# Layer 0 of a two-layer image network: another order of TensorE's work around the turning of sums and norm factors

## The chip, the core and the metric

The kernel runs on one core of a Trainium2 chip. The core has a matrix engine (PE, TensorE), a vector engine (DVE), an activation engine (ACT, ScalarE), a general engine (POOL, GpSimd) and an engine that mostly issues transfers (SP). Each works through its own queue of instructions in order; between queues, semaphores order the work. Matmul results land in PSUM[...]; everything else lives in SBUF or in DRAM. The metric is the device time of one execution in microseconds; the time given for a kernel is the median of its runs.

## The reference

The input is eight images of 256 channels on 32 by 32 pixels. Layer 0, which the change touches, does for each image:

```
a = attention(norm(x))         # 4 heads, key width 32, value width 64, over 1024 pixels
    qkv  = conv1x1, scaled     # 512 output channels: q 128, k 128, v 256
    attn = softmax(q . k / sqrt(32))
    out  = v . attn + depthwise 3x3 of v, scaled
    a    = conv1x1(out), scaled
x = x + gamma1 * a
f = edffn(norm(x))
    1024 hidden channels by conv1x1, depthwise 3x3, gelu(first 512) * (last 512)
    conv1x1 back to 256 channels
    8x8 patches: rfft2, times a filter, irfft2
x = x + gamma2 * f
```

Here norm divides by the root of the mean square over channels. Layer 1 is a causal attention and a mixture of eight experts over the pixels as tokens; it takes the larger half of the time and is left as it is.

## The kernel before

All of layer 0 stays in float32. An image is held as channels on 128 partitions, two blocks of channels by 1024 pixels (tile `t`, three buffers, so that three images are in flight). PE's work for image i is written out by hand as a generator, `main_of(i)` (line 1137), and every PE, DVE, ACT and POOL instruction of it is recorded by a helper (`InOrder`, line 60) that keeps each engine in the order of the program. That is why nearly all lines of the profile say L72.

Three images overlap. While PE runs the attention of image i, it also mixes and transforms the hidden layer of image i-2 (`spectrum`, line 1065), normalises image i-1 for its feed-forward part (`norm2`, line 917), opens the hidden channel groups of image i-1 (`open_group`, tiles `ph`, `hpad`, `x`, `conv`) and makes queries, keys and values of image i+1 (`queries_keys`, line 720; `values`, line 753). `weave(main, side, every)` (line 1118) lets a step of one generator follow every so many steps of another.

DVE's work beside this is the depthwise convolutions, tap by tap: those of the hidden groups, and ahead of them that of the values, `v_conv` (line 783), which writes the tile `o` (one buffer): ACT writes its middle tap, DVE adds eight more taps to each of two blocks. `level` (line 460) puts these steps between those of `main_of`: as soon as the recorded PE time of this image, times a share (0.95 for most images), exceeds the recorded DVE time, DVE steps follow. An estimate in the program thus decides where in the order they stand.

The pieces that the change touches:

- `attend` (line 793): four chunks of 256 queries, each in four steps. A step makes the scores `s` of two key blocks, ACT takes their exp (`pT`), and PE multiplies the exps of the step before with the values (`po`) and with ones (`sums`).
- `close` (line 819): when a chunk ends, ACT copies `po` to `pu` and the sums to `ss`. Then follow three steps on PE: `turn` (transposes `tps`; DVE takes the reciprocal `sr`, ACT copies it, POOL splits it in two parts `rs`), `back` (transposes `trs`; ACT copies to `rsT`) and `spread` (matmul `rb`; DVE multiplies `pu` and adds it to `o`). `later` (line 857) takes one of them at each step. The last chunk's steps are left to `finish` (line 894).
- `project` (line 900): the output projection `pp` of `o`, in two halves of 512 pixels, and DVE's addition of it into `t`. The second half's result is in the small PSUM buffers `ps_m` (two of them), which most small matmuls share.
- `rms_norm` (line 619): ACT squares `t` (`sq`), PE forms the mean squares (`ms`), ACT adds the constant (`yr`), PE turns them (`tpy`), POOL computes the factor in seven instructions (`a`, `y`, `r`), and after some empty steps (`gaps`) PE turns it back (`tr`) and spreads it (`rbn`); DVE then multiplies (`xn`).
- `spectrum`: four mixing matmul groups (`pz`), ACT copies (`zf`), transforms (`pf`, DVE's product `gf`, `py`) and DVE's addition into `t`. After the last, SP stores the finished `t` (`td`) and loads image b+3 into the same buffer.
- `gelu_steps` (line 1041): ACT's gelu of four groups, each followed by DVE's product `hid`.

Of the kernel before, what the change touches and what calls it, by code (L numbers as in the profile page):

```python
# [2 lines left out]

# [6 lines left out]
F32 = mybir.dt.float32  # L10
F32R = mybir.dt.float32r
AF = mybir.ActivationFunctionType
# [5 lines left out]
P = 128  # L18
# [9 lines left out]
QC = 256  # L28
# [76 lines left out]
def conv_attn_hybrid_kernel(  # L105
# [369 lines left out]
    act, pool = InOrder(tc, nc.scalar), InOrder(tc, nc.gpsimd)  # L475
    t = [None] * B
    with ExitStack() as l0:
        wpool = l0.enter_context(tc.tile_pool(name="w0", bufs=1))
        one = l0.enter_context(tc.tile_pool(name="one0", bufs=1))
        two = l0.enter_context(tc.tile_pool(name="two0", bufs=2))  # L480
# [108 lines left out]
        accs = keep.tile([P, 2, B, N // QC], F32, name="accs")  # L589
# [119 lines left out]
        xn2 = {}  # L709
# [83 lines left out]
        def attend(b):  # L793

            qst, kst, vT = (att[b][n] for n in ("qst", "kst", "vT"))
            nj = NT
            todo = []

            def product(po, sm, j, pT):


                for pair in range(NH // 2):
                    for i in range(4):
                        ch = pair * P + i * KD
                        pe.matmul(
                            po[i * KD : (i + 1) * KD, pair, :],
                            vT[:, j, ch : ch + KD],
                            pT[:, ch // HD, :],  # L810
                            start=(j == 0 and pair == 0),
                            stop=(j == nj - 1 and pair == 1),
                        )
                for hd in range(NH):
                    pe.matmul(
                        sm[hd * KD : (hd + 1) * KD, :], ones[:, :KD], pT[:, hd, :], start=(j == 0), stop=(j == nj - 1)
                    )

            def close(c, po, sm):
                pu = two.tile([P, NH // 2, QC], F32, tag="pu", name="pu", bufs=1)  # L820
                act.copy(pu, po)
                ss = two.tile([P, QC], F32, tag="ss", name="ss", bufs=1)
                act.activation(ss, sm, AF.Copy, accum_out=accs[:, 0, b, c : c + 1])
                qs = slice(c * QC, (c + 1) * QC)
                nt = QC // P
                of = {}

                def turn():
                    tp = ps_m.tile([P, nt, P], F32, tag="mm", name="tps")
                    for i in range(nt):  # L830
                        pe.transpose(tp[:, i, :], ss[:, i * P : (i + 1) * P], ident)
                    r = small.tile([P, nt, NH], F32, tag="sr", name="sr", bufs=2)
                    dve.reciprocal(r, tp[:, :, ::KD])
                    flat = r.rearrange("p a b -> p (a b)")
                    act.activation(flat, flat, AF.Copy, accum_out=accs[:, 1, b, c : c + 1])
                    rs = of["rs"] = small.tile([P, nt, 2, NH], F32, tag="rsp", name="rs", bufs=2)
                    pool.tensor_copy(rs[:, :, 0, :].bitcast(F32R), r)
                    pool.tensor_sub(rs[:, :, 1, :].bitcast(F32R), r, rs[:, :, 0, :])

                def back():  # L840
                    tr = ps_m.tile([2 * NH, QC], F32, tag="mm", name="trs")
                    for i in range(nt):
                        pe.transpose(tr[:, i * P : (i + 1) * P], of["rs"][:, i].rearrange("p a b -> p (a b)"), ident)
                    of["rT"] = small.tile([2 * NH, QC], F32R, tag="rsT", name="rsT", bufs=1)
                    act.copy(of["rT"], tr)

                def spread():
                    rb = ps_m.tile([P, NH // 2, QC], F32, tag="mm", name="rb")
                    for pair in range(NH // 2):
                        pe.matmul(rb[:, pair, :], pick_r[:, pair, :], of["rT"], start=True, stop=True)  # L850
                    o = att[b]["o"][:, :, qs]
                    dve.tensor_mul(pu, pu, rb)
                    dve.tensor_add(o, o, pu)

                return [None, turn, back, spread]

            def later():
                if todo:
                    step = todo.pop(0)
                    if step:  # L860
                        step()

            late = []

            def products():
                for one_ in late:
                    product(*one_[:4])
                    if one_[2] == nj - 1:
                        todo.extend(close(one_[4], *one_[:2]))
                late.clear()  # L870

            for c in range(N // QC):
                qs = slice(c * QC, (c + 1) * QC)
                po = ps_o.tile([P, NH // 2, QC], F32, tag="po", name="po")
                sm = ps_o.tile([P, QC], F32, tag="sm", name="sums")
                for j0 in range(0, nj, 2):
                    new = []
                    for j in (j0, j0 + 1):
                        ks = slice(j * P, (j + 1) * P)
                        s = ps_s.tile([P, NH, QC], F32, tag="s", name="s")  # L880
                        for hd in range(NH):
                            pe.matmul(s[:, hd, :], kst[:, hd, ks], qst[:, hd, qs], start=True, stop=True)
                        pT = two.tile([P, NH, QC], F32, tag="pT", name="pT", bufs=4)
                        act.activation(pT, s, AF.Exp)
                        new.append((po, sm, j, pT, c))
                    products()
                    late.extend(new)
                    later()
                    yield 3.5
            products()  # L890
            att[b]["rest"] = todo
            yield 2.6

        def finish(b):
            for step in att[b]["rest"]:
                if step:
                    step()
                yield 0.4

        def project(b, halves):  # L900
            for h in halves:
                hs = slice(h * HALF, (h + 1) * HALF)
                if h == 0:
                    both = ps_s.tile([P, KC, HALF], F32, tag="s", name="pp")
                    pps = [both[:, g, :] for g in range(KC)]
                else:
                    pps = [ps_m.tile([P, HALF], F32, tag="mm", name="pp") for _ in range(KC)]
                for g in range(KC):
                    conv1x1(pps[g], projw, g * P, att[b]["o"], hs)
                    yield 1.7  # L910
                for g in range(KC):
                    tb = t[b][:, g, hs]
                    dve.scalar_tensor_tensor(tb, pps[g], proj_o[:, g : g + 1], tb, ALU.add, ALU.add)

        def norm2(b):
            xn2[b] = one.tile([P, KC, N], F32, tag="xn2", name="xn2")
            yield from rms_norm(b, "n2w", xn2[b], 2)
            ready2[b] = True  # L920

        def group_tile(n):
# [195 lines left out]
        def weave(main, side, every, rest=True):  # L1118

            for n, us in enumerate(main):  # L1120
                yield us
                if n % every == every - 1:
                    step = next(side, None)
                    if step is not None:
                        yield step
            if rest:
                yield from side

        def none():
            yield from ()  # L1130

# [5 lines left out]
        def main_of(i):  # L1137

            steps = attend(i)
            if i >= 1:
                if i == 1:
                    yield from weave(norm2(i - 1), steps, 2, rest=False)
                else:
                    mixing = spectrum(i - 2)
                    yield from weave(norm2(i - 1), mixing, 1, rest=False)
                    yield from weave(mixing, steps, 2, rest=False)
            yield from weave(steps, queries_keys(i + 1) if i + 1 < B else none(), 1)  # L1150
            gelus = gelu_steps(i - 1) if i >= 1 else none()
            if i + 1 < B:
                stack(i + 1)
                yield from weave(values(i + 1), finish(i), 1)
                yield from weave(project(i, (0, 1)), gelus, 1)
            else:
                yield from weave(project(i, (0,)), weave(finish(i), gelus, 1), 1)
                yield from project(i, (1,))
# [813 lines left out]
```

## Time and profile before

| | us |
|---|---|
| median of 3 runs | 3170.32 (3169.82 to 3171.17) |
| the profiled execution | 3171.4 |
| its span in the profile | 3169.4 |
| layer 0 within it | about 0 to 1400 |
| one image of layer 0 (distance of equal instructions) | about 164.5 |

Names in the profile are those of the program's tiles, so `trs<-ident,rs` is a transpose of `rs` into `trs`. "PEld" is the loading of matmul weights, which runs beside matmuls. A row of the timeline has start, duration, engine, line, operation, output and inputs, and the number of records; in brackets stands how long the engine had been idle before it and what ended that. A row of the waits says which engine waited with what for whom: total, times, longest. A row of the windows gives, for a stretch of time, the busy time of PE, PEld, DVE, ACT and POOL, the granted clock of PE (1.00 is full), the DMA engines' busy share and GB/s.

### The profile page before, as it was taken

The page shows a single profiled execution, that of the slowest core. Times are in us where ns is not written, and L with a number is a line of the kernel's source. Part 1 is how long each engine was busy: PE and PEld are TensorE (multiplying, and loading weights), DVE is VectorE, ACT ScalarE, POOL GpSimd, SP SyncE. Part 2 cuts the span into 40 slices and gives each one's busy share as a digit, 9 for nine tenths or more (in the row PEclk, how much of TensorE's full clock was granted, in tenths as well). Part 3 has the DMA queues.
Part 4 walks back from the last instruction along what each step waited for, and adds up shares of the span by engine and source line. Part 5 has one row for each costly group of instructions (what it writes and reads, how often), then busy time and mean ns, then how long its engine had stood idle before and what let it go on. Part 6 is the DMA issues. An engine that isn't in the chain of part 4 may idle for free.

```text
span 3169.4 us, 41581 instructions
## 1 busy us (share of the span) xinstructions
PE 2933.1 (93%) x16802; PEld 1936.7 (61%) x16802; DVE 2390.7 (75%) x3014; ACT 1564.5 (49%) x2312; POOL 343.9 (11%) x422
## 2 busy tenths in 40 slices
PE   5998899899898989868999999899999999999998
PEld 3654555455555555445666666677777777777776
DVE  1378877878787869675767665588988888888887
ACT  1554445555454536323333333365666666666664
POOL 1121211111111110001122222100000000000000
PEclk9998999999999999989999999999999999999999
DMA  5213030212112020002423221411112142211210
GB/s 152 56 26 80 28 81 27 70 38 58 50 41 68 28 67 1 25 28 85 163 107 120 106 103 67 186 67 67 67 67 94 60 175 97 80 67 67 100 67 28
DMA packets 63599, 234.86 MB, mean 74 GB/s; under 512 B 5590, under 2 KB 13606, under 8 KB 54566
## 3 DMA queue, kind: packets, MB, share of 16 engines
q1 hardware_dynamic: 63094, 230.54, 21.8%
q8 instruction: 134, 2.20, 0.3%
q0 software_dynamic: 304, 1.57, 0.1%
q14 instruction: 67, 0.55, 0.1%
HBM read 140.61 MB, written 91.49 MB: 73 GB/s over the span
## 4 chain that ended last, share of the span: by engine, by line
PE 77%; DVE 14%; ACT 3%; POOL 2%; DMA 2%; issue 2%; SPq 0%; ACTq 0%; DVEq 0%; POOLq 0%
PE pm L72 12%; PE pa L72 11%; PE q L72 11%; PE po L72 10%; PE s L72 8%; PE ph L72 6%; DVE conv L72 3%; PE pq L72 3%; PE sums L72 3%; DVE o L72 2%; PE pz L72 2%; PE pv L72 2%; PE pk L72 2%; DVE x L72 1%; DVE zt L72 1%
## 5 line engine op out<-in xcount | busy, mean ns | idle before, releaser
L72 PE MATMUL pa<-ze,w 128*128 128x512 f32 x1488 | 423.2, 393 | 0.0
L72 DVE SCALAR_TENSOR_TENSOR x<-hpad,vec,x 128x1024 f32<-128x1024 f32 x248 | 317.0, 1282 | 41.0 <-ACT x L72 34.0
L72 DVE SCALAR_TENSOR_TENSOR conv<-hpad,vec,conv 128x1024 f32<-128x1024 f32 x256 | 330.1, 1296 | 13.8 <-ACT conv L72 7.3
L72 PEld LDWEIGHTS pa<-ze,w 128*128 128x128 f32 x1488 | 278.2, 188 | 63.3 <-issue 3.1
L72 ACT ACTIVATE h<-pa,bn_o,s1a 128x512 f32<-128x512 f32 x256 | 198.6, 776 | 203.6 <-PE pa L72 203.6
L72 ACT ACTIVATE pT<-s 128x1024 f32<-128x1024 f32 x256 | 247.4, 1024 | 71.7 <-PE s L72 71.7
L72 PE MATMUL po<-pT,vT 128*32 128x256 f32 x4096 | 273.3, 385 | 0.0
L72 PE MATMUL q<-h2p,w 128*128 128x512 f32 x768 | 269.0, 459 | 0.0
L72 DVE SCALAR_TENSOR_TENSOR h<-pa,s1b,h 128x512 f32<-128x512 f32 x256 | 191.2, 747 | 93.8 <-PE pa L72 86.0
L72 PE MATMUL ph<-xn,piw 128*128 128x512 f32 x512 | 244.9, 616 | 3.1 <-DVE xn L72 1.6
L72 PE MATMUL pm<-h,w 128*128 128x512 f32 x512 | 240.9, 593 | 0.0
L72 PE MATMUL s<-kk,z 128*128 128x512 f32 x512 | 236.8, 594 | 4.1 <-DVE pr L72 4.1
L72 PE MATMUL q<-z_first,w 128*128 128x512 f32 x768 | 217.2, 391 | 2.7 <-DVE z_first L72 1.7
L72 PE MATMUL pm<-h1p,w 128*128 128x512 f32 x768 | 216.7, 390 | 0.5 <-DVE h1p L72 0.5
L72 DVE SCALAR_TENSOR_TENSOR o<-vpad,pe_w,o 128x1024 f32<-128x1024 f32 x128 | 163.5, 1282 | 45.6 <-ACT o L72 42.4
L72 PEld LDWEIGHTS q<-h2p,w 128*128 128x128 f32 x768 | 144.6, 188 | 83.2 <-issue 59.6
L72 PE MATMUL s<-qst,kst 128*128 128x256 f32 x1024 | 176.2, 314 | 14.6 <-DMA kst<-part 13.2
L72 ACT ACTIVATE hpad<-ph,pi_o 128x512 f32<-128x512 f32 x126 | 86.9, 689 | 183.1 <-PE ph L72 176.1
L72 PEld LDWEIGHTS po<-pT,vT 128*32 128x32 f32 x4096 | 120.6, 110 | 85.5 <-issue 3.7
L72 PEld LDWEIGHTS s<-qst,kst 128*128 128x128 f32 x1024 | 137.6, 193 | 47.9 <-issue 42.9
L72 PEld LDWEIGHTS q<-z_first,w 128*128 128x128 f32 x768 | 144.4, 188 | 34.4 <-DVE z_first L72 2.9
L72 PEld LDWEIGHTS pm<-h1p,w 128*128 128x128 f32 x768 | 144.7, 189 | 31.7 <-DVE h1p L72 0.9
(271 smaller groups left out, 5066.1 us busy)
## 6 DMA issues: line engine op xcount, KB each, us to landing
ze<-zd SPq DMA_DIRECT2D x29, 1536.0 KB, 6.3
qst<-part SPq DMA_DIRECT2D x32, 512.0 KB, 6.9
kst<-part SPq DMA_DIRECT2D x32, 512.0 KB, 14.6
te<-ud SPq DMA_DIRECT2D x32, 512.0 KB, 4.1
wd<-parts_w SPq DMA_DIRECT2D x20, 768.0 KB, 3.8
w<-wd SPq DMA_DIRECT2D x20, 768.0 KB, 5.6
zd<-parts SPq DMA_DIRECT2D x14, 1024.0 KB, 3.9
t<-in_x_dram SPq DMA_DIRECT2D x8, 1024.0 KB, 7.5
```

What stands on the lines that cost most here:

```text
L72: return self._tc.keep_in_program_order(method(*args, **kwargs))
```

## The change

It changes order only; no matmul, copy or transfer is added or removed. In `close` the copy of the sums precedes that of `po`, and the empty first step goes. `later` takes a flag: a chunk's first step (`turn`) now stands ahead of the products of its attention step, the other two behind them as before. `norm2` of images 1 to 6 gets five empty steps in place of two where it runs beside `spectrum`, and three elsewhere. At the end of image i, the gelus stand among and ahead of the values, and the projection's first half follows the turning of the last sums; its second half moves into the start of image i+1, behind one step of squares and one mixing step (for i+1 = 1, behind one attention step). There norm and mixing alternate by a new helper, `some(steps, n)`, which takes n steps of a generator.

```diff
             def close(c, po, sm):
+                ss = two.tile([P, QC], F32, tag="ss", name="ss", bufs=1)
+                act.activation(ss, sm, AF.Copy, accum_out=accs[:, 0, b, c : c + 1])
                 pu = two.tile([P, NH // 2, QC], F32, tag="pu", name="pu", bufs=1)
                 act.copy(pu, po)
-                ss = two.tile([P, QC], F32, tag="ss", name="ss", bufs=1)
-                act.activation(ss, sm, AF.Copy, accum_out=accs[:, 0, b, c : c + 1])
...
-                return [None, turn, back, spread]
-
-            def later():
-                if todo:
-                    step = todo.pop(0)
-                    if step:
-                        step()
+                return [turn, back, spread]
+
+            def later(first):
+                if todo and (len(todo) == 3) == first:
+                    todo.pop(0)()
...
+                    early = len(todo) == 3
+                    later(True)
                     products()
                     late.extend(new)
-                    later()
+                    if not early:
+                        later(False)
...
-        def norm2(b):
+        def norm2(b, gaps=3):
             xn2[b] = one.tile([P, KC, N], F32, tag="xn2", name="xn2")
-            yield from rms_norm(b, "n2w", xn2[b], 2)
+            yield from rms_norm(b, "n2w", xn2[b], gaps)
...
+        def some(steps, n):
+            for us in itertools.islice(steps, n):
+                yield us
...
                 if i == 1:
+                    yield from some(steps, 1)
+                    yield from project(i - 1, (1,))
                     yield from weave(norm2(i - 1), steps, 2, rest=False)
                 else:
-                    mixing = spectrum(i - 2)
-                    yield from weave(norm2(i - 1), mixing, 1, rest=False)
+                    mixing, second = spectrum(i - 2), norm2(i - 1, 5)
+                    yield from some(second, 1)
+                    yield from some(mixing, 1)
+                    yield from project(i - 1, (1,))
+                    for _ in range(3):
+                        yield from some(second, 1)
+                        yield from some(mixing, 1)
+                    yield from weave(second, mixing, 1, rest=False)
                     yield from weave(mixing, steps, 2, rest=False)
...
             if i + 1 < B:
                 stack(i + 1)
-                yield from weave(values(i + 1), finish(i), 1)
-                yield from weave(project(i, (0, 1)), gelus, 1)
+                steps, ends = values(i + 1), finish(i)
+                yield from some(gelus, 2)
+                yield from some(steps, 2)
+                yield from gelus
+                yield from some(ends, 1)
+                yield from project(i, (0,))
+                yield from some(steps, 2)
+                yield from some(ends, 1)
+                yield from some(steps, 1)
+                yield from ends
+                yield from steps
```

`project` and `v_conv` are unchanged, and so is `level`, which runs `main_of(i)` with the value convolution and the hidden groups as its side.

More of the change, by code (lines that the diff above doesn't have):

```diff
@@ L1 @@
+import itertools
 import math
@@ L895, in finish @@
             for step in att[b]["rest"]:
-                if step:
-                    step()
+                step()
                 yield 0.4
```

## The prediction

> **What bounds the kernel now.** I read the shares of the page first, then PE's waits over the four equal images from 500 to 1158 us, then one image stage by stage, then the instructions around each gap in order of time.
>
> ```profile
> PE 2933.1 (93%) x16802; PEld 1936.7 (61%) x16802; DVE 2390.7 (75%) x3014; ACT 1564.5 (49%) x2312; POOL 343.9 (11%) x422
> ...
> PE trs L72 <- POOL rs L72: 35.5, 8, 5.9
> PE tr L72 <- DVE gf L72: 13.0, 4, 3.2
> ...
> 500.00:523.00 23.00, 18.52 (x129) 13.33 (x128) 19.27 (x25) 6.44 (x8) 3.94 (x6) 0.93 0.11 46
> 523.00:546.00 23.00, 23.00 (x224) 12.53 (x225) 18.37 (x15) 15.68 (x24) 0.00 (x0) 1.00 0.13 47
> 546.00:562.00 16.00, 12.98 (x127) 7.35 (x126) 13.94 (x13) 7.16 (x12) 8.83 (x9) 0.89 0.01 1
> 562.00:623.00 61.00, 61.00 (x621) 35.18 (x624) 49.89 (x49) 35.18 (x54) 3.98 (x4) 1.00 0.17 52
> 623.00:643.00 20.00, 12.93 (x47) 6.14 (x40) 12.44 (x12) 5.70 (x13) 5.92 (x6) 0.83 0.77 161
> ...
> 505.02 0.38 PE L72 MATMUL tr<-ident,r 128*8 128x128 f32 x2 [3.24 <-DVE gf L72]
> 505.24 5.30 PE L72 MATMUL pz<-pow__116,hid 128*128 128x256 f32 x16
> 557.18 0.59 PE L72 MATMUL trs<-ident,rs 128*8 128x128 f32 x2 [3.02 <-POOL rs L72]
> 557.57 4.80 PE L72 MATMUL ph<-xn,piw 128*128 128x512 f32 x8
> 623.34 3.70 PE L72 MATMUL pq<-xn,qkvw 128*128 128x512 f32 x8
> 634.34 0.59 PE L72 MATMUL trs<-ident,rs 128*8 128x128 f32 x2 [5.87 <-POOL rs L72]
> 634.73 5.47 PE L72 MATMUL pq<-xn,qkvw 128*128 128x512 f32 x8
> ```
>
> PE is the bound of layer 0: in the long middle stage (562 to 623) it is busy for all 61.00 us. It idles in three places of an image, 3.24, 3.02 and 5.87 us; with seven waits of 0.7 us or less an image loses 15.2 us. After each of the three the next group is slower: pq 5.47 against 3.70 for the same eight records, ph 4.80 against 3.70, pz 5.30 (3.62 undisturbed). That adds some 1.8, 1.1 and 1.5 us (pz is 4.80 in another image), so an image gives away about 19.6 of its 164.5 us. DVE is busy four fifths of the image and waits for PE in between.
>
> Two other chains, which cost nothing now, matter for what follows:
>
> ```profile
> 655.16 2.38 ACT L72 ACTIVATE o<-vpad,pe_o,pe_w 128x1024 f32<-128x1024 f32 x2
> 656.50 6.57 DVE L72 SCALAR_TENSOR_TENSOR o<-vpad,pe_w,o 128x1024 f32<-128x1024 f32 x5 [2.42 <-ACT o L72]
> ...
> 518.80 0.88 DVE L72 SCALAR_TENSOR_TENSOR t<-py,vec,t 128x256 f32<-128x256 f32 x2 [0.96 <-PE py L72]
> 519.71 0.34 SPq L1114 DMA_DIRECT2D td<-t  x1
> 523.76 0.40 SPq L487 DMA_DIRECT2D t<-in_x_dram  x1
> 528.68 1.15 ACT L72 ACTIVATE sq<-t 128x512 f32<-128x512 f32 x2 [0.76 <-DMA t<-in_x_dram]
> ```
>
> The first is the opening of the value convolution: ACT writes o (1.19 us a half), then DVE adds taps (1.31 us each). The second is the recycling of the tile t: finished image out, next image in, 9.0 us from the last DVE add (519.68) to the squares that need it. ACT waits only 0.76 us for it.
>
> [...] granted clock 0.50 from 634.3 to 638.0. It shows the loss after 3.0 us of idling too. [...]
>
> **The change, part by part.** Times are from the start of an image's first value projection (623.34 in the trace).
>
> *Turning sooner (close, later).* The copies pu and ss swap: ss is done about 0.4 us sooner. tps goes ahead of the products, about 2.7 us sooner. In the trace the 3.02 us wait ends with POOL's chain, on which rs queues behind the eight microseconds of norm factors begun at 547.74. In the new order that norm starts one attention step sooner and tr stands ahead of trs: from tpy to trs PE has 17 us of work; the factors and rs need about 13. So 3.02 + 1.1 = **4.1 us saved**. If rs stays late, nothing.
>
> *Gelus and half the projection among the values.* PE now has pq (3.5), tps (0.2), pp half (3.4), tpv (0.5), pq (3.5) ahead of trs: it arrives at 11.2. DVE does four taps (to 3.9), three hid products (4.0, the third not before its gelu at 6.5), then the reciprocal at 8.1; ACT 8.6; POOL 0.85 + 1.25 us: rs at 10.8. The wait of 5.87 and its 1.8 us clock loss go; the margin is only 0.4 us. Small waits there and at pz, 1.9 us before, come to about 1.3 (rb after rsT 0.3, tpv after its copies 1.0). **Saved 8.2 us.** The tables loaded stay two an image; gelus cost ACT the same, in time that it had idle.
>
> *Second half of the projection after the first mixing step.* This is the costly edit. After that step `level` has spent PE time, so it starts v_conv before the projection: o has one buffer, and the order of instructions becomes: PE pp (second half, reads old o); ACT writes new o, waiting for that pp; DVE five taps on new o; only then DVE's adds of pp into t; then PE's ms, whose PSUM buffer is that pp's. PE therefore stands for 0.3 + 1.19 + 0.15 + 6.57 + 0.74 = **8.9 us, plus 1.8 us of slow clock: 10.7 lost**. Before, both adds stood ahead of the taps. DVE has nothing else ahead of these taps, and ACT's next squares queue behind the o copies. What could hide it: nothing on PE, which keeps program order.
>
> *norm2 with five gaps.* tr moves behind two more transforms and one pz. The factors are there 8.4 us after tpy (495.90, POOL's last r ends at 504.34), and gf has freed its buffer by then; PE now has 11 us of work between. The 3.24 + 1.5 go: **4.7 saved**. Behind it tr, pf, rbn and py follow each other closely on two PSUM buffers: I count waits of 0.6, 0.3, 0.4 and 0.3 us against 1.0 now: 0.6 lost. The last py now stands ahead of the scores instead of between them, so the exp is less covered: 0.8 lost.
>
> *Squares of the next norm, moved with the attention steps.* They now follow directly on the first two exps in ACT's queue. From the first score matmul: last add into t ends at +1.2; td and t take 9.0: +10.2. Behind it on ACT: two squares (1.06), two exps (1.93), hpad and x of ph (1.36): +14.5. PE's ms waits for that x, since it takes ph's buffer; PE arrives at 3.4 + 2.8 + 3.6 = +9.8. So 4.7 us of waiting, and some 1.5 of clock: **6.2 lost**. Then ms still holds one of two buffers while two ph groups come in one go: the second waits for hpad and x of the first: **1.6 lost**.
>
> Sum for images 2 to 6: saved 4.1 + 8.2 + 4.7 = 17.0; lost 10.7 + 1.4 + 6.2 + 1.6 = 19.9; **2.9 us slower each**. Followed from end to end instead (old and new position of the fourth attention step, less the 4.1), I get 2.2; I take 2.5: 12.5 us for five.
> - Image 2 loses a longer wait now, 7.20 (1.3 more saved). In images 2 and 6 the recycling took 10.9 us, so the new wait grows by 1.9, of which about 1 is paid now already: 1.8 lost.
> - Image 1: the wait at tpy (3.83), about 2 us of clock and 0.9 of small waits go; the o chain with four taps costs 7.6 + 1.8: 2.7 lost.
> - Image 7: no next image, so no squares wait: 12.5 saved, 12.7 lost (six taps).
> - Tail of image 7: the reciprocal no longer sits behind hid and adds; trs 3.82 and part of pp's 2.91 go: 3.1 saved.
>
> Total: 12.5 - 1.3 + 1.8 + 2.7 + 0.2 - 3.1 = 12.8 us lost. The profiled execution took 3171.4 (span 3169.4), the runs' median 3170.32; the difference is added to the median: **3183 us**. Layer 1 is untouched.
>
> Costs that the trace doesn't show: clock loss after each new wait, 0 to 2.3 us (taken 1.8 and 1.5); the trs margin, 0 to 2 us lost (taken 0); recycling of t, 9.0 to 10.9. A gain below these is excluded, since each only lengthens a wait.
>
> **Rivals.**
> 1. *The squares' wait doesn't bite* (faster). If t lands within 5.5 us of the first score matmul instead of 10.2, the 6.2 us go in five images, and PE gains 31: 3183 - 31 = **3152**. For: today ACT waits only 0.76 us, and PE not at all. Against: store and load each took 4.0 us or more, and the last add stands just ahead of the scores. It decides where a norm or transform ends some 4 us sooner than I count. Chance 0.25.
> 2. *Savings and losses cancel*: my two sums differ by 0.7 an image; 2.5 less an image gives **3170**. Chance 0.20.
> 3. *Worse*: the trs margin fails (2 us in six images) and each recycling takes 10.9 (3 more images by 1.9): 3183 + 12 + 6 = **3201**. For: margin 0.4. Chance 0.13.
> The turning in attention not doing what it is placed for (POOL still late) belongs to 3: 4.1 in five images.
>
> **Numbers.** Forecast 3183: 0.42. 0.2% (6.3 us) is what a measurement can tell from no change. Faster 0.25, same 0.20, slower 0.42 + 0.13 = 0.55. Range 3148 to 3202: below rival 1 and above rival 3 by their unknowns. The forecast's own range is 3176 to 3194.
>
> **What would show it.** Right: no wait of trs on rs near 6 or 3 us, none of tr on gf; instead PE ms waiting about 9 us for DVE t in images 2 to 7, DVE o waiting some 8 us for ACT o, ACT sq waiting 6 us or more for the load, PE ms some 5 us. Wrong: a period under 164 us per image, or ms without a wait: then o is not reopened where I read it, or the load is early.

## The result, and the profile after

| | us |
|---|---|
| before, median of 4 runs | 3170.07 (3163.39 to 3171.17) |
| changed, median of 4 runs | 3191.34 (3190.24 to 3192.97) |
| ratio | 1.0067, 95% interval 1.0055 to 1.0079 |
| span of the profiled execution, before and changed | 3169.4 and 3191.1 |

The change makes the kernel 21 us slower: inside the range on record (3148 to 3202), 8 us above the forecast. The waits of PE over images 3 to 6 (us 500 to 1158) of the changed kernel; columns are total, times, longest:

```profile
PE ms L73 <- DVE t L73: 35.0, 4, 8.8
PE ms L73 <- ACT x L73: 18.4, 4, 4.8
PE ph L73 <- ACT x L73: 5.8, 4, 1.4
PE tpv L73 <- ACT vT L73: 2.7, 4, 0.7
```

The two heads of the same list before, trs on rs (35.5) and tr on gf (13.0), are gone. In their place stand two waits of ms, of 8.8 and up to 4.8 us. PE's busy time on the page, in which slowed matmuls count with their longer time (four records of ph 3.78 us after one of the waits below, 1.98 elsewhere), is what it was (2933.0 against 2933.1). So the added time is time in which PE stands.

The first wait is read in the timeline, all engines, of the changed kernel (start, duration, engine, line, operation, tiles, records; in brackets the idle time before and what ended it):

```profile
494.75 3.60 PE L73 MATMUL pp<-o,projw 128*128 128x512 f32 x8
...
498.39 2.37 ACT L73 ACTIVATE o<-vpad,pe_o,pe_w 128x1024 f32<-128x1024 f32 x2 [2.85 <-PE pp L73]
499.73 6.57 DVE L73 SCALAR_TENSOR_TENSOR o<-vpad,pe_w,o 128x1024 f32<-128x1024 f32 x5 [6.36 <-ACT o L73]
506.21 1.40 DVE L73 SCALAR_TENSOR_TENSOR t<-pp,proj_o,t 128x512 f32<-128x512 f32 x2
507.10 1.08 PE L73 MATMUL ms<-sq,ones 128*32 128x128 f32 x16 [8.76 <-DVE t L73]
508.12 4.65 PE L73 MATMUL pz<-pow__116,hid 128*128 128x256 f32 x16
```

Read it downwards: pp ends at 498.3, ACT may then overwrite o, DVE runs five taps on the new o, and only then the two adds that free pp's PSUM. PE stands from 498.3 to 507.1.

The second wait, a little later in the same image:

```profile
532.45 0.34 SPq L1115 DMA_DIRECT2D td<-t  x1
...
536.34 0.40 SPq L488 DMA_DIRECT2D t<-in_x_dram  x1
...
542.05 1.15 ACT L73 ACTIVATE sq<-t 128x512 f32<-128x512 f32 x2 [7.71 <-DMA t<-in_x_dram]
543.11 1.92 ACT L73 ACTIVATE pT<-s 128x1024 f32<-128x1024 f32 x2
544.92 0.69 ACT L73 ACTIVATE hpad<-ph,pi_o 128x512 f32<-128x512 f32 x1
545.49 0.79 ACT L73 ACTIVATE x<-ph,dw_o,vec 128x512 f32<-128x512 f32 x1
546.15 0.70 ACT L73 ACTIVATE hpad<-ph,pi_o 128x512 f32<-128x512 f32 x1
546.33 1.08 PE L73 MATMUL ms<-sq,ones 128*32 128x128 f32 x16 [4.83 <-ACT x L73]
```

ACT waits 7.71 us for the load with exps and evacuations behind it in its queue; ms, which needs ph's buffer, waits 4.83 us for the x at 545.49.

To see where the 21.7 us between the two spans arise, take the first pf after both ms matmuls in the head of an image as a mark; at it both kernels have done the same work. The forecast's terms are sorted by the same cuts:

| stretch | forecast | measured |
|---|---|---|
| start to the mark in image 2's head (328.03, 348.48) | 2.7 - 9.5 + 10.7 = +3.9 | +20.5 |
| from there to the mark in image 7's head (1153.77, 1180.64) | 5 x 2.5 + 1.8 = +14.3 | +6.4 |
| from there to layer 1's first pk (1437.34, 1455.48) | the rest, -5.4 | -8.7 |
| layer 1 | 0 | +3.6 |

The last row is no effect of an edit: first to last pk takes 507.9 us before and 511.2 after, and in the profiles of the kernels below either 507.9 to 508.5 or 511.3 to 511.8, the fastest kernel (511.3) among the latter. What makes the difference is not known.

The surplus of the first row is in image 1. Rows of its timeline, changed kernel:

```profile
231.89 3.78 PE L73 MATMUL ph<-xn,piw 128*128 128x512 f32 x4 [4.04 <-ACT x L73]
...
276.11 0.63 PE L73 MATMUL rbn<-rT,pick_n 8*128 8x128 f32 x4 [3.19 <-DVE sr L73]
...
317.19 0.38 PE L73 MATMUL trs<-ident,rs 128*8 128x128 f32 x2 [2.66 <-POOL rs L73]
```

With an earlier wait of s (2.16, at 170.4) these are 12 us of waits that the forecast has not, where before showed one of 1.58. All four are followed by slower matmuls: the granted clock over the next 4 us was 0.50 after s and ph, 0.73 after rbn and 0.71 after trs (ph took 3.78 for four records, 1.98 elsewhere).

### The profile page after: what moved, and what is told of

The parts are those of the page before. It is cut to its first block, busy times and chain, and to the rows that moved or that the text cites. A ratio compares the mean times of both kernels' runs of the same rounds, so it can differ in the third digit from the quotient of the medians.

```text
span 3191.1 us, 41551 instructions
## 1 busy us (share of the span) xinstructions
PE 2933.0 (92%) x16802; PEld 1944.7 (61%) x16802; DVE 2393.0 (75%) x3014; ACT 1563.0 (49%) x2312; POOL 324.6 (10%) x422
## 4 chain that ended last, share of the span: by engine, by line
PE 78%; DVE 13%; DMA 3%; ACT 3%; issue 1%; POOL 0%; SPq 0%; ACTq 0%; DVEq 0%; POOLq 0%
PE pm L73 12%; PE pa L73 11%; PE q L73 11%; PE po L73 10%; PE s L73 8%; PE ph L73 5%; PE pz L73 3%; PE pq L73 3%; DVE conv L73 3%; PE sums L73 3%; DVE x L73 3%; PE pv L73 2%; PE pk L73 2%; DVE o L73 2%; PE pp L73 2%; DVE zt L73 1%
## 5 line engine op out<-in xcount | busy, mean ns | idle before, releaser
L73 PE MATMUL s<-qst,kst 128*128 128x256 f32 x1024 | 186.1, 326 | 19.5 <-DMA kst<-part 13.3
L73 PEld LDWEIGHTS s<-qst,kst 128*128 128x128 f32 x1024 | 144.2, 202 | 63.1 <-issue 49.0
L73 PEld LDWEIGHTS ph<-xn,piw 128*128 128x128 f32 x512 | 90.8, 191 | 121.1 <-issue 87.5
```

The costliest lines, as they stand in the source:

```text
L73: return self._tc.keep_in_program_order(method(*args, **kwargs))
```

## The experiments

Twelve kernels were run in three groups, each beside the kernel before on the same chip (its medians there: 3172.79, 3170.34 and 3170.78 us). Ratios are to the kernel before, with the 95% interval. The changed kernel itself was not run again in these groups; a difference to its 3191.34 is therefore uncertain by some 3 us, by which the medians of the kernel before differ.

### The two new waits, one at a time and together

e1 lets the value convolution in only when the adds are queued:

```
                                         # in hidden():
     on_dve = [n for n in range(2 * ng) if n not in on_pe]
+    while b not in projected:
+        yield None
     for i, us in enumerate(lead):
...                                      # at the end of project()'s loop:
+    if h == 1:
+        projected.add(b)
```

> The changed kernel, but the value convolution of image i (ACT's write of o and the first taps) is let in only when both adds of the second projection half are in DVE's queue; nothing is left out. Theory A (the adds stand behind o's taps, and PE's ms behind the adds): the waits of ms on t of 7.4 to 10 us go in images 1 to 7, with some 1.8 us of slow clock each, so about 70 us: 3120. Theory B (DVE only starts its taps later, and the time comes back as waits of ph on x or of pz on hid): 3165 to 3180. Theory C (the ms wait is no cause, what slows the change is the wait of the next norm's squares for the load): 3185 to 3195.

e2 starts the next image's norm one attention step later:

```
-weave(steps, queries_keys(i + 1) if i + 1 < B else none(), 1)
+weave(steps, later_on(int(1 < i), queries_keys(i + 1)) if i + 1 < B else none(), 1)
```

> The changed kernel, but the next image's norm begins one attention step later in images 2 to 6; nothing is left out. Theory A: ACT's wait for the load of t no longer stands ahead of the x that frees ph's buffer, the ms wait on x of 4.7 us and its slow clock go in five images: 3160 to 3165. Theory B (the wait moves: the norm's factors or the queries come late at the end of the attention instead): 3180 to 3195.

e3 has both edits:

> Both edits together. Theory A, the two waits are independent: the gains of the two runs add, near 3090 to 3100, some 70 to 80 us faster than the kernel before. Theory B: less than the larger of the two single gains, since the same time is hidden once only.

e4 puts the second half of the projection back into its own image:

```
-yield from some(steps, 1)           # in the head of image 1
-yield from project(i - 1, (1,))     # in the heads of images 1 and of 2 to 7
...
 yield from steps                    # the end of values(i + 1)
+yield from project(i, (1,))
```

> The changed kernel, but the second half of the projection stands at the end of its own image again, behind the values, not in the head of the next; all else of the change stays. Theory A (the split of the projection over the image's border is the costly edit, because the value convolution opens between pp and its adds): the long ms waits go, a new wait of pp on DVE's o of 2 to 3 us comes, about 3140. Theory B: the place of the second half matters little, 3180 to 3195.

| | median | ratio |
|---|---|---|
| e1 | 3159.89 | 0.9963 (0.9951 to 0.9976) |
| e2 | 3184.71 | 1.0040 (1.0025 to 1.0054) |
| e3 | 3153.64 | 0.9947 (0.9930 to 0.9963) |
| e4 | 3166.39 | 0.9982 (0.9971 to 0.9993) |

Reopening o between pp and its adds is a cause: without it the changed kernel becomes faster than the one before. But e1 gained 31 us, not 70. PE's waits of e1 over all of layer 0 (us 60 to 1440), and DVE and PE around one of them:

```profile
PE py L73 <- DVE gf L73: 24.3, 12, 4.8
PE ms L73 <- ACT x L73: 23.4, 5, 5.0
```

```profile
488.93 10.53 DVE L73 SCALAR_TENSOR_TENSOR o<-vpad,pe_w,o 128x1024 f32<-128x1024 f32 x8 [2.06 <-ACT o L73]
...
499.37 0.68 DVE L73 TENSOR_TENSOR gf<-pf,filt 128x512 f32<-128x512 f32 x1
...
500.11 2.08 PE L73 MATMUL py<-idft,gf 128*128 128x128 f32 x8 [3.64 <-DVE gf L73]
```

No ms wait on t is left (61.3 us in seven in the changed kernel), but the taps must run somewhere. Eight of them now stand ahead of gf, and py waits: 24.3 us in twelve waits, against 1.4 in the changed kernel. Theory A is right about the cause; the time came in below theory B's range, but part of it does come back, as B says, though at py and not at ph or pz. The marks show where: e1 is 19.9 us ahead at the mark in image 2's head (328.63), gains 5.4 us an image from there to image 7's head, and gives 11.8 us back behind that.

e2 removed the ms wait on x altogether and gained only 7 us. In its place, images 3 to 6:

```profile
PE ms L73 <- DVE t L73: 35.0, 4, 8.8
PE trs L73 <- POOL rs L73: 19.1, 4, 4.8
```

The time is theory B's, by a wait that it didn't name. The wait of trs in attention is back, and longer than before the change (3.02): the norm's factors again stand on POOL ahead of the sums' split. That wait had gone because the norm began early, which is what made ACT wait for the load. With the norm one step earlier or later, one of the two waits is there. The gains of e1 and e2 do add (38 us in e3), but each is far smaller than theory A of e3 took it (3090 to 3100).

e4 lies between its two theories. The long ms waits are gone and pp waits for o as foreseen (2.1 us an image), but tr waits for gf again: 12.9 us in four waits of images 3 to 6, as before the change. Of the 25 us to the changed kernel, all are there at the mark in image 2's head (322.97); from there to image 7's head e4 gains only 0.5 us an image.

### The start of image 1, and the turning alone

e5 restores the border between images 0 and 1:

```
 if i == 1:
-    yield from some(steps, 1)
-    yield from project(i - 1, (1,))
     yield from weave(norm2(i - 1), steps, 2, rest=False)
...
 yield from steps                    # the end of values(i + 1)
+if i == 0:
+    yield from project(i, (1,))
```

> The changed kernel, but at the border between images 0 and 1 the second half of the projection stays at the end of image 0, and image 1 begins with its norm, as before; nothing is left out. In the changed kernel's trace image 1 lost some 16 us that the prediction didn't count: waits of ph on x (4.0), rbn on sr (3.2), s (2.2), trs on rs (2.7). Theory A: they come from the moved half (DVE begins its taps early and the hidden groups bunch): they go together with the first ms wait (7.4) and its slow clock, 3170 to 3175. Theory B: they come from turning sooner or from the new end of image 0, only the ms wait goes and the wait at tpy (3.8) returns: 3185 to 3188.

3180.5 us, ratio 1.0032 (1.0021 to 1.0044), between the two theories. Its mark in image 2's head is at 336.21, 12.3 us ahead of the changed kernel's. The waits of rbn on sr and of s are gone, ph's on x and trs's shrink to 1.4 and 0.6, and the wait at tpy (3.8) is back; new are 2.8 of ph on pu and 5.0 of pz on hid. So moving the half projection over this border causes most of image 1's surplus, by the hidden groups' order behind it as well as by o: e1, without the o wait, still shows ph waiting 4.0 and rbn 3.2.

e7 is the changed kernel with close and later as before; e12 is the kernel before with the new close and later:

```
 def close(c, po, sm):               # e12; e7 is the reverse
-    act.copy(pu, po)
     act.activation(ss, sm, ...)
+    act.copy(pu, po)
...
+early = len(todo) == 3
+later(True)
 products()
 late.extend(new)
-later()
+if not early:
+    later(False)
```

> The changed kernel, but sums are copied and turned in attention as before (pu ahead of ss, tps behind the products and one step later); the rest of the change stays. Theory A (turning sooner itself saves the wait of trs on rs that the kernel before had in attention): a wait of 3 to 5 us returns in five images, 3205 to 3215. Theory B (the wait went because the next norm begins sooner, and its factors are through POOL before the sums are turned): no trs wait returns, 3185 to 3195.

> The kernel before with one edit of the change alone: sums copied and turned sooner. Nothing is left out. Theory A (turning sooner brings rs sooner and saves the wait of trs of 3.0 us in attention with its slow clock): 3145 to 3155. Theory B (POOL's queue decides: rs still stands behind the norm's factors, PE only arrives at trs earlier, and the wait stays or grows to the 4.8 us of the changed kernel with later squares): 3168 to 3182.

e7: 3189.48 us, ratio 1.0060 (1.0043 to 1.0076): the same time as the changed kernel, and no wait of trs in attention in images 2 to 6. e12: 3181.34, ratio 1.0029 (1.0019 to 1.0038): turning sooner alone makes the kernel slower. Both are theory B. POOL's queue there, with DVE's reciprocal and PE, e12:

```profile
714.11 2.53 POOL L72 TENSOR_TENSOR a<-y,mhalf 128x8 f32<-128x8 f32 x1 [43.41 <-ACT y L72]
715.05 0.20 DVE L72 RECIPROCAL sr<-tps 128x8 f32<-128x8 f32 x1
716.72 2.32 POOL L72 TENSOR_TENSOR y<-y,a 128x8 f32<-128x8 f32 x2
...
724.53 1.11 POOL L72 TENSOR_TENSOR rs<-sr,rs 128x8 fp32r<-128x8 f32 x1
...
725.70 0.59 PE L72 MATMUL trs<-ident,rs 128*8 128x128 f32 x2 [4.63 <-POOL rs L72]
```

The reciprocals are ready for POOL at 716.1, when ACT has copied them; rs starts at 724.27, when seven instructions of the norm's factors are through. Turning sooner does not make rs ready sooner; PE only comes to trs earlier and waits 4.63 us in place of 3.02.

### The other two parts alone

e8 is the kernel before with the new end of an image, and both halves of the projection in it:

```
-yield from weave(values(i + 1), finish(i), 1)
-yield from weave(project(i, (0, 1)), gelus, 1)
+steps, ends = values(i + 1), finish(i)
+yield from some(gelus, 2)
+yield from some(steps, 2)
+yield from gelus
+yield from some(ends, 2)            # the empty first step, and turn
+yield from project(i, (0,))
+yield from some(steps, 2)
+yield from some(ends, 1)
+yield from some(steps, 1)
+yield from ends
+yield from steps
+yield from project(i, (1,))
```

> The kernel before with the change's order at the end of an image alone (gelus and the first half of the projection among the values, the second half behind the values of the same image); turning in attention, norm2's steps and the head of the next image are as before. Theory A (the prediction's 8.2 us an image saved by it, in seven images, less a new wait of pp on o of some 2.5): 3172 less 40: about 3130. Theory B (PE's waits there only move to pp and ph, because DVE's hid products now stand ahead): 3160 to 3175.

3133.18 us, ratio 0.9888 (0.9869 to 0.9907): 37 us faster than before, as theory A has it. Its waits in images 3 to 6:

```profile
PE tr L73 <- DVE gf L73: 13.0, 4, 3.2
PE trs L73 <- POOL rs L73: 12.1, 4, 3.0
PE pp L73 <- DVE o L73: 5.6, 4, 1.4
```

The wait of trs among the values (5.87) is gone and costs 1.4 us of pp instead; those of tr and of trs in attention stay as they were.

e11 is the kernel before with five empty steps in norm2:

```
-yield from rms_norm(b, "n2w", xn2[b], 2)
+yield from rms_norm(b, "n2w", xn2[b], 5 if 1 <= b < B - 1 else 2)
```

> The kernel before with one edit of the change alone: norm2 of images 1 to 6 gets five empty steps in place of two, which also uses up the mixing steps between which attention began, so that the next norm's squares follow the first two exps. Nothing is left out. Theory A (the prediction's terms: the wait of tr on gf goes, 4.7 us, and that of trs on rs in attention with it, 4.1, since the next norm starts a step sooner; the wait of ms on x comes, 6.2, and the second ph, 1.6, and 1.4 of small ones): within 5 us of 3170. Theory B (the new wait weighs more than both savings, as the comparison of the kernel with the new image end alone, 3133, and the changed kernel with the second half put back, 3166, suggests): 3190 to 3205.

3202.12 us, ratio 1.0099 (1.0078 to 1.0120): theory B. This edit alone costs 31 us. It moves tr and, by using up mixing steps, also begins the next norm one attention step sooner; e11 doesn't separate the two. Waits in images 3 to 6:

```profile
PE trs L72 <- POOL rs L72: 19.7, 4, 4.9
PE ms L72 <- ACT x L72: 17.2, 4, 4.6
PE tr L72 <- DVE gf L72: 12.9, 4, 3.2
```

The four waits of trs are those among the values. The one in attention is gone here with the old turning; in e2, with the five steps and a later norm, it is there. So the earlier norm takes it away. The wait of tr on gf, for which the steps seem to be put in, is there unchanged. The kernel before, and then e11 at the same place, show why:

```profile
664.31 0.68 DVE L72 TENSOR_TENSOR gf<-pf,filt 128x512 f32<-128x512 f32 x1
664.91 3.79 DVE L72 SCALAR_TENSOR_TENSOR o<-vpad,pe_w,o 128x1024 f32<-128x1024 f32 x3
...
668.62 0.68 DVE L72 TENSOR_TENSOR gf<-pf,filt 128x512 f32<-128x512 f32 x1
...
669.45 0.58 PE L72 MATMUL tr<-ident,r 128*8 128x128 f32 x2 [3.24 <-DVE gf L72]
```

```profile
676.65 1.13 POOL L72 TENSOR_TENSOR r<-a,r 128x8 fp32r<-128x8 f32 x1
...
679.02 3.92 DVE L72 SCALAR_TENSOR_TENSOR o<-vpad,pe_w,o 128x1024 f32<-128x1024 f32 x3
...
682.86 0.68 DVE L72 TENSOR_TENSOR gf<-pf,filt 128x512 f32<-128x512 f32 x1
...
683.68 0.38 PE L72 MATMUL tr<-ident,r 128*8 128x128 f32 x2 [3.23 <-DVE gf L72]
```

The last thing that tr waits for is PSUM that gf must empty, and gf stands behind three taps on o. Before, the factors come only 0.5 us sooner than gf (r ends at 668.76, gf at 669.30). In e11 they have been there for 5.1 us when gf starts, but tr, now further back, needs the buffer of the next gf, and three more taps stand ahead of that one. This debt of taps is paid at tr (before, e4, e11), at py (e1), or under the wait of ms (the changed kernel); putting tr further back does not change it.

### Two versions that go further

e9 is e8 with the split of the reciprocal on DVE instead of POOL:

```
-pool.tensor_copy(rs[:, :, 0, :].bitcast(F32R), r)
-pool.tensor_sub(rs[:, :, 1, :].bitcast(F32R), r, rs[:, :, 0, :])
+dve.tensor_copy(rs[:, :, 0, :].bitcast(F32R), r)
+dve.tensor_sub(rs[:, :, 1, :].bitcast(F32R), r, rs[:, :, 0, :])
```

> The kernel before with the change's image end alone (3133 us before), and DVE in place of POOL splits the sums' reciprocal into rs. Nothing is left out. Theory A (the wait of trs on rs in attention is POOL's queue, on which rs stands behind the norm's factors): 20 us of waits and some 8 of slow clock go, about 3108. Theory B (DVE's taps ahead of the split take POOL's place, or two more short instructions a chunk delay DVE): 3125 to 3140.

3119.46 us, ratio 0.9837 (0.9819 to 0.9855), the fastest, between the two theories. No trs wait is left in images 3 to 6; pp's on o grows from 5.6 to 10.4 us there, as DVE has 64 instructions more (2404.4 us busy, 2391.3 in e8).

e10 adds norm2's five steps to it, with the next norm held back by one attention step:

> As the run before it in this list, and norm2 of images 1 to 6 gets the change's five empty steps, with the next norm held where it was (one attention step later than the empty steps alone would put it). Theory A: the wait of tr on gf (3.2 us, with some 1.5 of slow clock) goes in six images without the wait of ms on x: some 25 us below that run, near 3085. Theory B (attention has one step less beside the mixing, and the exps are less covered): equal to it within 6 us.

3133.40 us, ratio 0.9884 (0.9865 to 0.9903): 14 us slower than e9, outside both theories. tr waits as before (12.9 in images 3 to 6); what it loses is clock, below.

e6 is e3 with two further edits: at most two DVE steps after each PE step, and the next norm two attention steps later.

> The version with o's taps held until the adds, and two further edits: at most two DVE side steps follow each step of PE's order (the held kernel showed py waiting 3.6 and more on gf behind a burst of eight taps), and the next norm begins two attention steps later, so that POOL splits the sums ahead of the norm's factors (the held kernel with the norm one step later showed trs waiting 4.8 us on rs). Theory A: both waits go, some 5.5 and 6.5 us with clock in five to six images, 3153 less 60: near 3095. Theory B: DVE, held back by the cap, is late for the hidden groups at the end of the image (pz on hid, ph on x), and the queries come out of the attention's cover: 3140 to 3165.

3218.64 us, ratio 1.0152 (1.0135 to 1.0169), the slowest, beyond both theories: trs waits on rs 47.6 us in all (up to 9.8), pf on gf 15.9. These waits of trs are not those of attention. There the later norm does bring rs ahead of the factors, and neither trs nor ms on x waits in images 2 to 6; trs waits among the values, because DVE comes late to the reciprocal:

```profile
555.67 1.13 POOL L73 TENSOR_TENSOR rs<-sr,rs 128x8 fp32r<-128x8 f32 x1
556.75 1.63 POOL L73 TENSOR_TENSOR a<-y,mhalf 128x8 f32<-128x8 f32 x1
...
636.17 5.24 DVE L73 SCALAR_TENSOR_TENSOR conv<-hpad,vec,conv 128x1024 f32<-128x1024 f32 x4
...
642.52 0.20 DVE L73 RECIPROCAL sr<-tps 128x8 f32<-128x8 f32 x1
...
645.32 0.59 PE L73 MATMUL trs<-ident,rs 128*8 128x128 f32 x2 [7.56 <-POOL rs L73]
```

tps ended at 630.5; taps and products of the hidden groups stand ahead of sr until 642.5. That fits theory B's reason, DVE held back by the cap. e6 has two edits beyond e3, and no run has the norm two steps later without the cap.

### Standing and clock, image by image

For images 2 to 6 (mark to mark, five images), profiled executions. "Clock lost" adds up, over windows of 5 us, one minus the granted clock times 5 us; "PE idle" is the window less PE's busy time in it. All are us per image, and somewhat rough, since missing records count as idle, and since the clock can be low during a wait, where it costs nothing (0.52 from 503.00 to 507.10 in the changed kernel, where PE stood throughout). The profiled execution of e8 was 5.5 us faster than its median, that of e4 4.1 us slower.

| | per image | PE idle | clock lost |
|---|---|---|---|
| before | 165.1 | 15.7 | 6.5 |
| changed | 166.4 | 17.7 | 8.2 |
| e1, o held | 161.1 | 13.2 | 3.8 |
| e4, second half back | 165.9 | 12.1 | 12.3 |
| e8, image end alone | 158.4 | 10.2 | 5.1 |
| e9, and split on DVE | 155.7 | 8.5 | 4.1 |
| e10, and five steps | 158.4 | 8.0 | 7.8 |
| e11, five steps alone | 170.1 | 16.8 | 10.9 |
| e12, turning alone | 167.4 | 16.4 | 7.2 |

e4, e10 and e11 have norm2's five steps without the long wait of ms on t. Their idle time says little; they lose by the clock. PE's busy time an image (the first column less the second), which slowed matmuls lengthen, says the same: 153.3 us in e11 against 149.4 before, and 150.4 in e10 against 147.2 in e9, which over five images is 16 us, about the whole difference between these two. The list of waits shows nothing of this.

## Why the prediction was right, and where it was not

The direction and the range hold, and both new waits came where and as long as forecast. What these waits are worth, and why two old ones went, was in part read wrongly. Each step in turn:

- **Second half in the next image's head: right.** Forecast a wait of 8.9 us of ms on t; measured 8.76 in images 2 to 6, by the very chain described (7.4 in image 1; 10.1 in image 7, with six taps). Its worth was overrated: forecast 10.7 lost an image, but holding o (e1) returned 31 us in seven images, about 4.5 each, and putting the half back (e4) only 0.5 an image in images 2 to 6. The step took it that nothing on PE hides these taps, and did not ask where they would run otherwise: they are the same taps behind which gf waits.
- **Squares of the next norm: the wait was right** (forecast 4.7; measured 4.26 to 4.83; ph 1.6, measured 1.4). Rival 1, that it does not bite, falls. Taking it away by a later norm is worth 7 us, not some 30, since the wait of trs returns (e2).
- **Turning sooner, 4.1 saved: the wait went, and by the cause given, but not by this edit.** The prediction rests the saving on the norm that begins one attention step sooner. e11, with that and norm2's steps alone, has no such wait, and e2, with a later norm, has it back; e7 and e12 show that turning sooner saves nothing, and alone costs 11 us. So the saving belongs to the same move as the squares' wait.
- **norm2 with five gaps, 4.7 saved: the wait went, but the reason was wrong.** This is the step whose mechanism failed. "gf has freed its buffer by then" holds for one gf, but tr comes to need the next one's: e11 and e4 keep the wait of 3.2. In the changed kernel it went because taps had been run under the wait of ms. Saved was counted here what is paid there.
- **Gelus and half the projection among the values, 8.2 saved: right in mechanism.** The 5.87 went and the margin of 0.4 us held in images 2 to 6. e8 gives 37 us over seven image ends, 5.3 each, with the 1.4 us that pp waits.
- **Image 1, 2.7 lost: the term that was most mis-sized.** Measured +20.5 at the first mark against +3.9. The ledger kept the savings at tpy and at the last trs and counted the half projection's wait, but no wait of ph, rbn or s behind it. e5 gives 12.3 us of it back.
- **Clock, 1.5 to 1.8 a wait: right in the sum, but no constant.** The forecast's clock terms come to 1.1 us less an image (4.4 saved with three old waits, 3.3 lost with two new). PE's busy time an image fell by 0.7 (165.1 - 15.7 to 166.4 - 17.7), though the sum of lost clock, which counts waits too, rose from 6.5 to 8.2. Single waits of 3.2 us lost from nothing to 6.5 us (last section).

The errors partly cancel: images 2 to 6 lost less than forecast (6.4 against 14.3) and the last stretch gained more (8.7 against 5.4), while image 1 lost 16.6 more. That the sum came within 8 us, 3.6 of which are layer 1's, is in part luck. (Image 7's saving of 12.5 is not worked out in the prediction; its terms 8.2 and 4.7 give 12.9. Of its tail, the wait of pp on o grew from 2.9 to 4.5 where part of it was to go.) Rival 2, that savings and losses cancel, is nearly true of images 2 to 6 taken alone.

What stays open: which order within image 1 makes its hidden groups bunch (no run took that apart), why e5 regains 12.3 us at the mark but 11 in the median, and what e6 would do without its cap.

## What to carry to other kernels

A wait that goes with an edit has not been saved by it until it is known which work ended it and where that work runs now: here one burst of taps on DVE stalled PE at tr, at ms or at py, depending on the order. Test every part of a reordering alone: the part that pays (the new image end, 37 us) was hidden by others that cost (31 us for the five steps, 11 for the turning, 25 for the moved half, the last measured within the change; they don't simply add). And before work is turned sooner, look at what stands ahead of it in its engine's queue: taking two short instructions out of POOL's queue gave the 14 us from e8 to e9, which turning sooner could not.

## What was not expected of the hardware

Behind waits of tr of one length, 3.2 us, the clock lost from nothing to 6.5 us. Windows about the end of such a wait (columns: PE, PEld, DVE, ACT and POOL busy with instructions, granted clock, DMA share, GB/s): first before (the wait ends at 669.45), where a dense group of pz follows, then e11 (683.68), where short groups of pf, rbn and py follow, the first after a gap of 0.45 us, then e9 (643.50), with pz as before:

```profile
669.40:673.40 4.00, 3.95 (x13) 3.23 (x14) 3.93 (x5) 0.36 (x1) 0.00 (x0) 0.60 0.00 0
673.40:677.40 4.00, 3.47 (x17) 2.16 (x15) 2.46 (x4) 1.87 (x2) 0.00 (x0) 1.00 0.00 0
```

```profile
684.00:688.00 4.00, 3.55 (x9) 1.87 (x9) 1.42 (x3) 1.65 (x2) 0.00 (x0) 0.58 0.02 4
688.00:692.00 4.00, 3.98 (x18) 3.60 (x17) 3.23 (x6) 0.00 (x0) 0.00 (x0) 0.50 0.00 0
692.00:696.00 4.00, 3.66 (x19) 3.16 (x18) 3.31 (x5) 1.94 (x2) 0.00 (x0) 0.64 0.39 164
```

```profile
642.00:646.00 4.00, 2.50 (x13) 2.25 (x14) 3.96 (x6) 0.36 (x1) 0.81 (x1) 1.00 0.00 0
646.00:650.00 4.00, 3.46 (x17) 2.15 (x15) 3.93 (x5) 1.87 (x2) 0.00 (x0) 1.00 0.00 0
```

One wait cost 1.6 us of clock (0.40 x 4.0), one 5.1 (0.42, 0.50 and 0.36 of 4.0), one nothing. All such waits, one each in the heads of images 2 to 7, fall apart in this way, with the lost clock summed over the 14 us behind each. In before, e8, e9 and e12, where pz follows, the 24 waits lost 1.6 to 1.7 us, but nothing in four cases, and 2.8 to 2.9 in image 7. In e4, e10 and e11, with norm2's five steps, the 18 waits lost 3.4 to 6.5. The wait is 3.2 us in all of them, so its length does not make the difference. The order around tr goes with it; which of its groups matters, no run takes apart.

In e8 and e9, waits with the same length and the same work behind them lost 1.7 us or nothing; what decides between the two is not shown. In e11, from 688 to 692, PE counts as busy for 3.98 of 4.00 us, and the clock stays at 0.50. Why it stays low there is open.

POOL's short instructions took unlike times beside unlike work of DVE. The two products y took 0.48 us together in the kernel before (from 714.64), where DVE had just stood idle for 1.74 us, and 2.32 in e12 (from 716.72), where DVE ran taps throughout. The four instructions behind them took 1.05 to 1.25 us each in the kernel before (from 715.21), beside taps, and 0.19 to 0.20 in the changed kernel from 519.11 on, while DVE was at gf and t. No run separated DVE's work from other causes.
